# Moving the mask tables, the statistics steps and the fetch depth in the convolution layer of a fused kernel

## The chip, the cores and the metric

The kernel runs on one core of one Trainium2 chip. The metric is the device time of one execution in microseconds (us); lower is better. A core has four compute engines with a queue of instructions each: PE (TensorE, matmuls; its weight loads are listed as PEld), DVE (VectorE), ACT (ScalarE) and POOL (GpSimd). A fifth queue, SP, issues the transfers between DRAM and the core's own memory (SBUF). Matmul results land in banks of a memory of their own (PSUM). Each queue is worked through in the order in which it was built; an instruction whose input or buffer is not ready waits, and what stands behind it waits too.

## The reference

The input x is 128 images x 128 channels x 16 x 16, float32. Two layers are computed:

```
gn(v): group norm, 32 groups of 4 channels
bn(v): batch norm over batch and both image axes
aq(v): round(clip(v, 0, 1) * 15) / 15
# layer 0
h = aq(bn(gn(x)))
h = conv3x3(h, quantised(w1) * cross)           # 5 taps differ from 0
h = aq(bn(h))
h = conv3x3(h, quantised(w2) * diagonal)        # 5 taps differ from 0
x = x + (h + gn(x))
# layer 1, on tokens (16*16 per image, 128 channels)
t = tokens(x)
t = t + mamba(layernorm(t)) + reversed(mamba(reversed(layernorm(t))))
t = t + experts(layernorm(t))                   # 8 experts, the best 2 of each token
```

The mamba has 4 heads and works in chunks of 64 tokens. Inside a chunk it needs a triangular mask, forward and backward. The kernel builds that mask into a small matmul of two tables, `rows` and `cols`, which are constants.

## The kernel before, in words

The images are taken in pairs: one pair is a tile of 128 channels x 2 images x 256 positions, 256 KB, and there are NP = 64 pairs (B = 128 images). Layer 0 comes in three stages, and layer 1 follows as the main stage. The engines' instructions in the layer 0 stages are put in order by a scheduler when the program is built: it simulates when each operand is ready by costs of its own and lets each engine take what is ready first. `issue_after` is a hint to it to hold an instruction back behind another. The main stage has its order written out by hand as a schedule of steps. All loads and stores named here are issued by SP.

**Setup (0 to 87 us).** The first weights w1 are loaded, then all 64 pairs into `xr` (L371), which stay in SBUF through layer 0; after them the weights of layer 1 (`load_weights`, L278 to 307) and w2 (L400, 401). Each image's mean and variance per channel come from `bn_stats` on DVE (L443); every fourth image is instead done by ACT, a sum first (L441) and a sum of squares about the mean later (L457, which needs the mean from L453 to 455). The images are cut into four groups, `cuts` (L414): 0 to 48, 48 to 96, 96 to 120 and 120 to 128. After a group's statistics come small steps on 128 x (images of the group) values: L462 to 468 make the mean and variance of each image and channel, a matmul with `grp` (L472, a table made in L347 to 355) averages over the 4 channels of a norm group, L473 to 476 and a second matmul (L478) make the group variance, L480 adds epsilon and L481 takes the square root on ACT. `normed` (L420 to 434) takes the reciprocal, makes one Newton step and leaves the scale and shift of the group norm; it is called for a group after the statistics of the next. All these small steps are DVE's, but for two in `normed` (L431, L432, GpSimd's: `ares` and `bres`, by which x is scaled in the second convolution). L495 to 511 fold group norm and batch norm into one scale `sc1` and one shift `bi1` for each image and channel.

In the same stage GpSimd makes the two constant tables: `rows0` by 8 copies and `cols0` by 4 copies and 8 selections (`patterns`, L376 to 397, called in L488). L489 and L490 store them to DRAM as `rows_d` and `cols_d` (each 128 x 2048 bf16, 512 KB), from where `constants` (L695 to 698) loads them, three times each, at the beginning of the main stage. The buffers of `rows0` and `cols0` belong to the pool `setup1`, whose space is used by the q buffers of the next stage.

**First convolution (87 to 169 us).** For each pair: ACT or GpSimd makes q = xr * sc1 + bi1 (L525, 527), DVE clips it and writes it as integers into one of four padded images `hpad` (L192, in `quantise`), PE makes 5 matmuls of 128 x 512 (L218, in `conv3x3`), ACT copies the result (L541), DVE takes its statistics for the second batch norm (L542), and SP stores it (L544). The first 8 pairs are not stored but kept in SBUF. `by_weights` (L223) looks at the quantised weights and branches to one of three versions of the stage; with these weights it is the one with 5 taps and one matmul for each.

**Second convolution (169 to 293 us).** For each pair: SP fetches the first result from DRAM (`fetch`, L615 to 618, 6 buffers, issued 5 pairs ahead), ACT scales it (L622) and DVE writes the padded image (L192), PE makes 5 matmuls (L218), the two images in xr are scaled by GpSimd (L665; of every fourth pair one image by ACT, L663), DVE adds the two (L666). `stored` (L625 to 635) transposes the pair before on PE (L631), ACT copies the result to `yt` (L633, 3 buffers) and SP stores it (L635, to y, for layer 1); the first 4 pairs are kept in SBUF instead. The loop is at L649 to 674. Some steps of layer 1's weights (`second_weights`, L309 to 342, with matmuls in L318) and of its first layernorm (`early`, L637 to 645, with ACT's L600) are put between.

**Main stage (293 us to the end).** Mamba and experts. The change does not touch its code.

Of the kernel before, what the change touches and what calls it, by code (L numbers as in the profile page):

```python
# [8 lines left out]
F32 = mybir.dt.float32  # L9
BF16 = mybir.dt.bfloat16  # L10
AF = mybir.ActivationFunctionType
ALU = mybir.AluOpType
AX = mybir.AxisListType

P = 128
NT = 256
# [5 lines left out]
NH = 4  # L22
HD = 64
# [11 lines left out]
def kernel(ctx: ExitStack, tc: tile.TileContext, a: dict):  # L35

    nc = tc.nc
    x_d, out_d = a["x"], a["out"]
    B = x_d.shape[0]
    NP = B // 2  # L40
# [19 lines left out]
    rows_d = dram.tile([P, NH, 2, 2, P], BF16, name="rows_d")  # L60
# [248 lines left out]
    def second_weights(pool, psw):  # L309
# [31 lines left out]
        nc.vector.tensor_scalar(aneg, aneg, -1.0, None, ALU.mult)  # L341
        yield

    with tc.tile_pool(name="w1p", bufs=1) as w1p:

        grp = w1p.tile([P, P], F32, name="grp")
# [5 lines left out]
            out=grp, in_=grp, pattern=[[4, 32], [0, 4]], compare_op=ALU.is_ge, fill=0.0,  # L352
            base=3, channel_multiplier=-1,
        )
        nc.vector.tensor_scalar(grp, grp, 0.25, None, ALU.mult)
        sc1 = w1p.tile([P, B], F32, name="sc1")
        bi1 = w1p.tile([P, B], F32, name="bi1")
        wq1 = w1p.tile([P, 9, 3, P], BF16, name="wq1")
# [1 line left out]
        with tc.tile_pool(name="setup1", bufs=1) as setup, tc.tile_pool(  # L360
# [8 lines left out]

            for i in range(NP):  # L370
                nc.sync.dma_start(xr[i], x_c[:, 2 * i : 2 * i + 2, :])  # L371
            rows0 = setup.tile([P, NH, 2, 2, P], BF16, name="rows0")
            cols0 = setup.tile([P, 2, 2, 2, 2, P], BF16, name="cols0")
            far = setup.tile([HD, 1], BF16, name="far")

            def patterns():  # L376
                nc.gpsimd.memset(far, -1e30)
                for h in range(NH):
                    nc.gpsimd.tensor_copy(
                        rows0[:, h].rearrange("p d t l -> p (d t l)"), heads[:, h : h + 1].to_broadcast([P, 4 * P])  # L380
                    )
                    nc.gpsimd.tensor_copy(
                        rows0[0:HD, h].rearrange("p d t (f l) -> p (d t f) l", l=HD),
                        ident[0:HD, 0:HD].unsqueeze(1).to_broadcast([HD, 2 * 2 * 2, HD]),
                    )
                for m in range(2):
                    for d in range(2):
                        sign = 1 - 2 * d
                        nc.gpsimd.tensor_copy(
                            cols0[:, m, d].rearrange("p j f l -> p (j f l)"), triple[:, m : m + 1].to_broadcast([P, 4 * P])  # L390
                        )
                        for half in range(2):
                            nc.gpsimd.affine_select(
                                out=cols0[0:HD, m, d, :, half, :], in_=far.unsqueeze(2).to_broadcast([HD, 2, P]),
                                pattern=[[0, 2], [sign, P]], compare_op=ALU.is_ge, fill=0.0,
                                base=-sign * HD * half - 1, channel_multiplier=-sign,
                            )

            load_weights()
            w2 = w1p.tile([P, 9, P], F32, name="w2", tag="w")  # L400
            nc.sync.dma_start(w2, a["L0_conv_w2"])


            bst = setup.tile([P, B, 6], F32, name="bst")
# [6 lines left out]
            mean, var, dm, gm, dev, qv, ga, neg, shift = (  # L411
                tb(n) for n in ("mean", "var", "dm", "gm", "dev", "qv", "ga", "neg", "shift")
            )
            cuts = [0, 3 * B // 8, 3 * B // 4, B - max(B // 16, 1), B]  # L414

            def by_scalar(b):

# [2 lines left out]
            def normed(c):  # L420

                of = slice(cuts[c], cuts[c + 1])
                var_, gm_, dev_, ga_, qv_, dm_ = (t[:, of] for t in (var, gm, dev, ga, qv, dm))
                nc.vector.reciprocal(ga_, ga_)
                nc.vector.tensor_tensor(dm_, ga_, ga_, ALU.mult)
                nc.vector.tensor_tensor(dm_, dm_, qv_, ALU.mult)
                nc.vector.tensor_scalar(dm_, dm_, -0.5, 1.5, ALU.mult, ALU.add)
                nc.vector.tensor_tensor(ga_, ga_, dm_, ALU.mult)
                nc.vector.scalar_tensor_tensor(shift[:, of], gm_, -1.0, ga_, ALU.mult, ALU.mult)
                nc.gpsimd.tensor_scalar(ares[:, of], ga_, 1.0, SCALE, ALU.add, ALU.mult)  # L430
                nc.gpsimd.tensor_scalar(bres[:, of], shift[:, of], SCALE, None, ALU.mult)  # L431
                nc.vector.tensor_tensor(dev_, dev_, ga_, ALU.mult)  # L432
                nc.vector.tensor_tensor(var_, var_, ga_, ALU.mult)
                nc.vector.tensor_tensor(var_, var_, ga_, ALU.mult)

            for c in range(4):
                of = slice(cuts[c], cuts[c + 1])
                for b in range(B)[of]:
                    x_b = xr[b // 2][:, b % 2, :]
                    if by_scalar(b):  # L440
                        nc.scalar.activation(junk, x_b, AF.Copy, accum_out=bst[:, b, 1:2])  # L441
                    else:
                        behind = nc.vector.bn_stats(bst[:, b, :], x_b)  # L443
                if c > 0:

                    with tc.issue_after(behind.ins):
                        normed(c - 1)
                mean_, var_, dm_, gm_, dev_, qv_, ga_ = (t[:, of] for t in (mean, var, dm, gm, dev, qv, ga))
                mine = [b for b in range(B)[of] if by_scalar(b)]
                if mine:  # L450

                    picked = slice(mine[0], cuts[c + 1], 4)
                    nc.vector.tensor_scalar(neg[:, picked], bst[:, picked, 1], -1.0 / NT, None, ALU.mult)  # L453
                    nc.vector.tensor_scalar(bst[:, picked, 1], neg[:, picked], -1.0, None, ALU.mult)
                    nc.vector.tensor_scalar(bst[:, picked, 4], neg[:, picked], -1.0, None, ALU.mult)
                    for b in mine:
                        nc.scalar.activation(  # L457
                            junk, xr[b // 2][:, b % 2, :], AF.Square, bias=neg[:, b : b + 1],
                            accum_out=bst[:, b, 2:3],
                        )  # L460

                nc.vector.tensor_tensor(mean_, bst[:, of, 1], bst[:, of, 4], ALU.add)  # L462
                nc.vector.tensor_scalar(mean_, mean_, 0.5, None, ALU.mult)
                nc.vector.tensor_tensor(dm_, bst[:, of, 1], bst[:, of, 4], ALU.subtract)
                nc.vector.tensor_tensor(dm_, dm_, dm_, ALU.mult)
                nc.vector.tensor_tensor(var_, bst[:, of, 2], bst[:, of, 5], ALU.add)
                nc.vector.tensor_scalar(dm_, dm_, 0.25, None, ALU.mult)
                nc.vector.scalar_tensor_tensor(var_, var_, 1.0 / NT, dm_, ALU.mult, ALU.add)

                n = cuts[c + 1] - cuts[c]  # L470
                gm_ps = psa.tile([P, 512], F32, name=f"gm_ps{c}", tag="gm_ps", bufs=2)[:, :n]
                nc.tensor.matmul(gm_ps, grp, mean_, start=True, stop=True)  # L472
                nc.vector.tensor_copy(gm_, gm_ps)  # L473
                nc.vector.tensor_tensor(dev_, mean_, gm_, ALU.subtract)
                nc.vector.tensor_tensor(qv_, dev_, dev_, ALU.mult)
                nc.vector.tensor_tensor(qv_, qv_, var_, ALU.add)
                gv_ps = psa.tile([P, 512], F32, name=f"gv_ps{c}", tag="gv_ps", bufs=2)[:, :n]
                nc.tensor.matmul(gv_ps, grp, qv_, start=True, stop=True)  # L478

                nc.vector.tensor_scalar(qv_, gv_ps, EPS, None, ALU.add)  # L480
                nc.scalar.activation(ga_, qv_, AF.Sqrt)  # L481
                if c == 0:
                    for _ in range(5):
                        next(weights)
                if c == 1:
                    for _ in weights:
                        pass
                    patterns()  # L488
                    nc.sync.dma_start(rows_d, rows0)  # L489
                    nc.sync.dma_start(cols_d, cols0)  # L490
                if c == 3:
                    normed(c)

            bm = setup.tile([P, 1], F32, name="bm")
            nc.vector.tensor_reduce(bm, dev, AX.X, ALU.add)  # L495
# [109 lines left out]
    def conv2(taps, nq):  # L605
        with tc.tile_pool(name="pc", bufs=6) as pc, tc.tile_pool(
# [7 lines left out]

            def fetch(i):  # L615
                if NP > i and i not in kept:
                    qs[i] = pc.tile([P, 2, NT], F32, name=f"q2_{i}", tag="q")
                    nc.sync.dma_start(qs[i], o1_d[i])

            def quantised(i):  # L620
# [16 lines left out]
            def early(i):  # L637
# [6 lines left out]
                nc.scalar.copy(uTs[i], u_ps)  # L644
                yield

            early_steps = [step for i in range(2) for step in [early(i)] * 5]

            for i in range(5):  # L649
                fetch(i)  # L650
            for i in range(3):
                quantised(i)
            for i in range(NP):
                b = 2 * i
                fetch(i + 5)
                if i + 3 < NP:
                    quantised(i + 3)
                ps = psc.tile([P, 2, NT], F32, name=f"cv2_{i}", tag="cv")
# [9 lines left out]
                stored(i - 1)  # L668
                if i >= NP // 2 and early_steps:
                    next(early_steps.pop(0))  # L670
                if i % max(NP // 8, 1) == max(NP // 8, 1) - 1:
                    with tc.issue_after(behind.ins):
                        next(weights, None)
            stored(NP - 1)
            for step in early_steps:
                next(step)
            for _ in weights:
# [634 lines left out]
```

## Time and profile before

| | us |
|---|---|
| median of 3 runs | 2557.53 |
| the 3 runs | 2561.13, 2553.94, 2557.53 |
| the profiled execution | 2554.94 |
| its span, first to last instruction | 2553.1 |

The granted TensorE clock of the profiled execution is 0.991. Busy time of the engines in the stages, in us, with the mean busy share of the 16 DMA engines and what they moved:

| stage, us of the span | PE | DVE | ACT | POOL | DMA share | GB/s |
|---|---|---|---|---|---|---|
| setup, 0 to 87.3 | 6.13 | 65.79 | 42.18 | 23.91 | 0.78 | 237 |
| first convolution, 87.3 to 168.8 | 77.82 | 74.87 | 67.07 | 56.87 | 0.48 | 177 |
| second convolution, 168.8 to 293 | 108.45 | 85.62 | 92.08 | 72.55 | 0.74 | 250 |
| main stage, 293 to 2553 | 2222.88 | 2026.88 | 1971.63 | 1475.98 | 0.41 | 121 |

How to read the lines of the profile that follow. A line of the *timeline* is: start in us, length in us, engine, code line, operation, output<-input with shapes, how many instructions the line stands for, and in brackets the idle time of the engine ahead of it with what ended that. SPq is SP's queue issuing transfers. A line of the *waits* is: engine, what waited and its code line, what it waited for, then the sum of the waits in us, how many, and the longest. The *chain of work that ended last* is followed back from the last instruction, at each step to what released it.

### The profile page before, as it was taken

The numbers are of one execution on the slowest core, as the hardware profiler recorded it, in microseconds if no ns is written. First come the engines' busy times: TensorE is split into PE (matmuls) and PEld (weight loads), VectorE is DVE, ScalarE is ACT, GpSimd is POOL, SyncE is SP. The second block draws the span as 40 slices with busy tenths as digits, with TensorE's granted clock in tenths as the row PEclk, the third lists the DMA queues.
The fourth block names the chain that finished last, engine by engine and source line by source line (L and its number), as shares of the span: only waits on it lengthen the run. The fifth ranks groups of instructions, "written<-read, shape, count | busy, mean of one in ns | idle before, by whom it ended". The sixth has DMA issues, their size and how long they took to land.

```text
span 2553.1 us, 49290 instructions
## 1 busy us (share of the span) xinstructions
PE 2415.3 (95%) x15940; PEld 1479.9 (58%) x15940; DVE 2253.2 (88%) x6163; ACT 2173.0 (85%) x4455; POOL 1629.3 (64%) x1694
## 2 busy tenths in 40 slices
PE   0688889999999999999999999999999999999997
PEld 0235456666666666666666666666666666666663
DVE  8787699999999999999999999999999999999883
ACT  5678699888889998889898888998988899898881
POOL 3468026676666666666666666666667666666666
PEclk9999899999999999999999999999999999999998
DMA  9358633434444444444444344444433443443343
GB/s 287 124 192 281 227 67 110 125 111 123 130 124 122 122 125 118 120 132 128 120 126 124 114 119 129 128 121 119 129 118 117 132 132 121 123 123 116 107 125 107
DMA packets 302167, 339.58 MB, mean 133 GB/s; under 512 B 56768, under 2 KB 226752, under 8 KB 301888
## 3 DMA queue, kind: packets, MB, share of 16 engines
q1 hardware_dynamic: 301888, 336.21, 43.3%
q8 instruction: 133, 2.18, 0.3%
q14 instruction: 146, 1.20, 0.2%
HBM read 262.72 MB, written 56.62 MB: 125 GB/s over the span
## 4 chain that ended last, share of the span: by engine, by line
PE 88%; DMA 4%; DVE 3%; ACT 2%; issue 1%; SPq 1%; POOL 1%; POOLq 0%; ACTq 0%; DVEq 0%
PE f_ps L1189 17%; PE x_ps L877 13%; PE y_ps L1012 10%; PE z_ps L920 9%; PE o_ps L1072 9%; PE sg L965 5%; PE xt_ps L932 4%; PE y_ps L1018 4%; PE g_ps L951 4%; PE cv L218 4%; DMA xr<-in_x 2%; PE n_ps L1045 1%; PE u_ps L1094 1%; PE f_ps L1184 1%; PE u_ps L750 1%
## 5 line engine op out<-in xcount | busy, mean ns | idle before, releaser
L1177 POOL TENSOR_TENSOR gb<-gb,u2T 128x512 f32<-128x512 f32 x512 | 641.3, 1277 | 122.7 <-PE y_ps L1018 68.8
L895 DVE SCALAR_TENSOR_TENSOR xc<-x_ps,cw,xc 128x510 f32<-128x510 f32 (+2 forms) x768 | 571.7, 744 | 46.5 <-ACT xc L889 36.9
L1028 POOL TENSOR_TENSOR yg<-yg,z 128x512 f32<-128x512 f32 x256 | 325.9, 1279 | 352.1 <-DVE yg L1024 155.1
L1189 PE MATMUL f_ps<-gb,ew 128*128 128x512 f32 x1024 | 510.1, 602 | 6.7 <-POOL gb L1177 6.4
L877 PE MATMUL x_ps<-uT,wx 128*128 128x512 f32 x768 | 402.9, 607 | 7.6 <-ACT e L731 3.3
L731 ACT ACTIVATE e<-sg 128x512 f32<-128x512 f32 x512 | 299.3, 591 | 49.9 <-PE sg L965 44.4
L731 ACT ACTIVATE e<-e,ends 128x128 f32<-128x128 f32 x1024 | 325.0, 392 | 0.0
L1012 PE MATMUL y_ps<-e,xt 128*64 128x256 f32 x2048 | 317.8, 389 | 0.2 <-DVE yg L1024 0.2
L993 DVE TENSOR_TENSOR e<-e,g_ps 128x1024 f32<-128x1024 f32 x256 | 311.6, 1217 | 5.5 <-ACT e L731 2.4
L895 DVE SCALAR_TENSOR_TENSOR bc<-x_ps,cw,bc 128x510 f32<-128x510 f32 (+2 forms) x384 | 286.7, 747 | 20.5 <-ACT bc L889 4.1
L1189 PEld LDWEIGHTS f_ps<-gb,ew 128*128 128x128 f32 x1024 | 180.5, 192 | 174.2 <-issue 136.2
L920 PE MATMUL z_ps<-uT,wz 128*128 128x512 f32 x512 | 271.2, 611 | 1.5 <-ACT xc L889 1.0
L889 ACT ACTIVATE xc<-x_ps,cb,cw 128x512 f32<-128x512 f32 x256 | 199.0, 777 | 64.0 <-PE x_ps L877 57.4
L1072 PE MATMUL o_ps<-wo,yg 128*128 128x128 f32 x2048 | 251.4, 276 | 0.2 <-DVE e L998 0.2
L1072 PEld LDWEIGHTS o_ps<-wo,yg 128*128 128x128 f32 x2048 | 240.5, 193 | 11.1 <-DVE g L1149 8.4
L1024 DVE SCALAR_TENSOR_TENSOR yg<-xc,dcol,y_ps 128x512 f32<-128x512 f32 x256 | 189.8, 742 | 50.1 <-PE y_ps L1018 46.8
L1060 POOL TENSOR_TENSOR rr<-rr,mhalf 128x8 f32<-128x8 f32 x64 | 109.9, 1718 | 161.7 <-DVE g L1151 82.7
L1018 PE MATMUL y_ps<-e,xt 128*64 128x128 f32 x2048 | 199.0, 273 | 0.0
L965 PE MATMUL sg<-rows,cols 128*128 128x256 bf16 x1024 | 192.1, 274 | 5.8 <-ACT e L731 2.8
L1018 PEld LDWEIGHTS y_ps<-e,xt 128*64 128x64 f32 x2048 | 147.0, 137 | 74.1 <-DVE e L998 0.5
L218 PE MATMUL cv<-hpad,wq 128*128 128x512 bf16 x640 | 161.7, 396 | 19.5 <-DVE hpad L192 19.4
L1012 PEld LDWEIGHTS y_ps<-e,xt 128*64 128x64 f32 x2048 | 118.9, 136 | 100.9 <-issue 53.8
(256 smaller groups left out, 4813.9 us busy)
## 6 DMA issues: line engine op xcount, KB each, us to landing
gb<-gd SPq DMA_DIRECT2D x256, 512.0 KB
e<-cum SPq DMA_DIRECT2D x256, 256.0 KB
xr<-in_x SPq DMA_DIRECT2D x64, 256.0 KB
cc<-bc SPq DMA_DIRECT2D x128, 128.0 KB
out<-ob SPq DMA_DIRECT2D x64, 256.0 KB
y<-yt SPq DMA_DIRECT2D x60, 256.0 KB
yt<-y SPq DMA_DIRECT2D x60, 256.0 KB
o<-o SPq DMA_DIRECT2D x56, 256.0 KB
```

Of the source, the lines that this page charges most:

```text
L731: nc.scalar.activation(out, in_, func, **more)
L877: nc.tensor.matmul(ps, wx[d][:, n * P : (n + 1) * P], uTs[i], start=True, stop=True)
L895: nc.vector.scalar_tensor_tensor(acc[:, :, to], raw[:, :, of], cw[:, d, n, 3 - back : 4 - back], acc[:, :, to], ALU.mult, ALU.add,)
L920: nc.tensor.matmul(ps, wz[:, d, n * P : (n + 1) * P], uTs[i], start=True, stop=True)
L965: nc.tensor.matmul(sg[:, :, of], c_[:, k, d, s, half, :], r_[:, :, d, s, of], start=True, stop=True)
L993: nc.vector.tensor_tensor(e0.rearrange("p h t l -> p h (t l)"), e0.rearrange("p h t l -> p h (t l)"), gps[i, d, k][:, 0:NT].unsqueeze(1).t ...
L1012: nc.tensor.matmul(y_ps[64 * q : 64 * q + 64, k, :], xt[:, 2 * k + s0, 64 * h : 64 * h + 64], e0[:, h].rearrange("p t l -> p (t l)"), star ...
L1018: nc.tensor.matmul(y_ps[64 * q : 64 * q + 64, k, s1 * P : (s1 + 1) * P], xt[:, 2 * k + s1, 64 * h : 64 * h + 64], e1[:, h, :], start=False ...
L1028: large(nc.gpsimd.tensor_tensor(yg, yg, zs[i, d][:, n, :], ALU.mult))
L1072: nc.tensor.matmul(o_ps[:, (2 * j + d) * P : (2 * j + d + 1) * P], ygs[i, d, n][:, t * P : (t + 1) * P], wo[d][:, n, :], start=(n == 0), s ...
L1177: large(nc.gpsimd.tensor_tensor(gb[:, e], gb[:, e], u2Ts[i], ALU.mult))
L1189: nc.tensor.matmul(f_ps, ew[:, e, :], gbs[i, e], start=False, stop=(e == NE - 1))
```

## The change

Four things are changed.

1. `patterns` becomes a generator that takes a pool. It is no longer called in the setup, but in the second convolution: from pair 32 on, one of its steps is put into the program after each pair, and what is left after the last pair. Its three tables (`rows0`, then `cols0` in two halves) use one buffer in turn (tag "table", bufs=1), so that the stores are now one of 512 KB to `rows_d` and two of 256 KB to `cols_d`, each of which must have read the buffer before the next table is made.
2. The small steps of the first batch norm are issued by GpSimd for the first three groups, by DVE for the last; the copy of the group means out of PSUM (L473) by ACT for the first three groups. Two `scalar_tensor_tensor` instructions become two instructions each. The scaling of `grp` goes to GpSimd. `normed` is called directly after each group. The third bound of `cuts` goes from image 120 to 112.
3. The q buffers of the second convolution go from 6 to 10, and the fetches from 5 to 8 pairs ahead.
4. The load of w2 is issued ahead of `load_weights` instead of behind it.

```diff
+    def patterns(pool):
+        far = pool.tile([HD, 1], BF16, name="far", bufs=1)
+        nc.gpsimd.memset(far, -1e30)
+        rows0 = pool.tile([P, NH, 2, 2, P], BF16, name="rows0", tag="table", bufs=1)
+        for h in range(NH):
+            nc.gpsimd.tensor_copy(
+                rows0[:, h].rearrange("p d t l -> p (d t l)"), heads[:, h : h + 1].to_broadcast([P, 4 * P])
+            )
+            yield
+            nc.gpsimd.tensor_copy(
+                rows0[0:HD, h].rearrange("p d t (f l) -> p (d t f) l", l=HD),
+                ident[0:HD, 0:HD].unsqueeze(1).to_broadcast([HD, 2 * 2 * 2, HD]),
+            )
+            yield
+        nc.sync.dma_start(rows_d, rows0)
+        for m in range(2):
+            cols0 = pool.tile([P, 2, 2, 2, P], BF16, name=f"cols0_{m}", tag="table", bufs=1)
+            for d in range(2):
+                sign = 1 - 2 * d
+                nc.gpsimd.tensor_copy(
+                    cols0[:, d].rearrange("p j f l -> p (j f l)"), triple[:, m : m + 1].to_broadcast([P, 4 * P])
+                )
+                yield
+                for half in range(2):
+                    nc.gpsimd.affine_select(
+                        out=cols0[0:HD, d, :, half, :], in_=far.unsqueeze(2).to_broadcast([HD, 2, P]),
+                        pattern=[[0, 2], [sign, P]], compare_op=ALU.is_ge, fill=0.0,
+                        base=-sign * HD * half - 1, channel_multiplier=-sign,
+                    )
+                    yield
+            nc.sync.dma_start(cols_d[:, m], cols0)
...
-        nc.vector.tensor_scalar(grp, grp, 0.25, None, ALU.mult)
+        nc.gpsimd.tensor_scalar(grp, grp, 0.25, None, ALU.mult)
...
-            load_weights()
             w2 = w1p.tile([P, 9, P], F32, name="w2", tag="w")
             nc.sync.dma_start(w2, a["L0_conv_w2"])
+            load_weights()
...
-            cuts = [0, 3 * B // 8, 3 * B // 4, B - max(B // 16, 1), B]
+            cuts = [0, 3 * B // 8, 3 * B // 4, 7 * B // 8, B]
+            half_ = setup.tile([P, B], F32, name="half_")
...
+                eng = nc.vector if c == 3 else nc.gpsimd
                 nc.vector.reciprocal(ga_, ga_)
-                nc.vector.tensor_tensor(dm_, ga_, ga_, ALU.mult)
...
+                eng.tensor_tensor(dm_, ga_, ga_, ALU.mult)
...
-                if c > 0:
-
-                    with tc.issue_after(behind.ins):
-                        normed(c - 1)
...
-                    nc.vector.tensor_scalar(neg[:, picked], bst[:, picked, 1], -1.0 / NT, None, ALU.mult)
+                    nc.gpsimd.tensor_scalar(neg[:, picked], bst[:, picked, 1], -1.0 / NT, None, ALU.mult)
...
-                nc.vector.tensor_tensor(mean_, bst[:, of, 1], bst[:, of, 4], ALU.add)
+                eng.tensor_tensor(mean_, bst[:, of, 1], bst[:, of, 4], ALU.add)
...
-                nc.vector.tensor_copy(gm_, gm_ps)
+                (nc.vector.tensor_copy if c == 3 else nc.scalar.copy)(gm_, gm_ps)
...
-                    patterns()
-                    nc.sync.dma_start(rows_d, rows0)
-                    nc.sync.dma_start(cols_d, cols0)
-                if c == 3:
-                    normed(c)
+                normed(c)
...
-                    qs[i] = pc.tile([P, 2, NT], F32, name=f"q2_{i}", tag="q")
+                    qs[i] = pc.tile([P, 2, NT], F32, name=f"q2_{i}", tag="q", bufs=10)
...
+            tables = patterns(pc)
...
-            for i in range(5):
+            for i in range(8):
                 fetch(i)
...
-                fetch(i + 5)
+                fetch(i + 8)
...
+                if i >= NP // 2:
+                    with tc.issue_after(behind.ins):
+                        next(tables, None)
...
             stored(NP - 1)
+            for _ in tables:
+                pass
```

The other lines of the diff send further small steps of `normed` and of the group loop, in the same way, to `eng`.

## The prediction

> **What bounds the kernel now.** I read the page first. PE is busy 95% of the span and the chain of work that ended last is 88% PE, nearly all of it in the main stage, which the change does not touch: from 293 us on, the instructions of all engines are the same in both built programs, apart from two memsets that change places. So I read the 293 us ahead of it: the chain and the timeline from 65 to 92 us for the join of batch norm and first convolution (conv1), then waits, GpSimd's and the DMA queue's timelines from 178 to 293 us for the second convolution (conv2).
>
> ```profile
> 11.14 7.84 DVE L355 TENSOR_SCALAR grp<-grp 128x128 f32<-128x128 f32 x1
> 17.43 1.48 POOL L393 TENSOR_SCALAR_AFFINE_SELECT cols<-far 64x256 bf16<-64x256 bf16 x4
> ...
> 77.33 0.29 DVE L511 TENSOR_SCALAR bi<-bi,b 128x128 f32<-128x128 f32 x1
> 79.74 0.43 SPq L489 DMA_DIRECT2D rows_d<-rows  x1
> 85.72 3.23 ACT L525 ACTIVATE q<-xr,bi,sc 128x256 f32<-128x256 f32 x6 [13.64 <-DMA rows_d<-rows]
> 87.33 4.97 PE L218 MATMUL cv<-hpad,wq 128*128 128x512 bf16 x13 [11.41 <-DVE hpad L192]
> ```
>
> The scale and shift for conv1 are ready at 77.62, but its first q tile lies where the tables lay, and waits until they are copied out at 85.72. Between them 8.1 us are lost; PE starts at 87.33.
>
> ```profile
> ACT q L622 <- DMA q<-o: 13.7, 16, 1.5
> PEld yt_ps L631 <- ACT yt L633: 9.6, 13, 1.2
> ```
>
> These waits of conv2 say that its image pairs come late from DRAM.
>
> ```profile
> 177.77 35.92 POOL L665 TENSOR_SCALAR xr<-xr,ares,bres 128x256 f32<-128x256 f32 x59 [4.39 <-issue]
> ...
> 216.30 4.36 POOL L665 TENSOR_SCALAR xr<-xr,ares,bres 128x256 f32<-128x256 f32 x7
> ...
> 222.36 0.55 POOL L665 TENSOR_SCALAR xr<-xr,ares,bres 128x256 f32<-128x256 f32 x1
> ...
> 223.26 25.52 POOL L665 TENSOR_SCALAR xr<-xr,ares,bres 128x256 f32<-128x256 f32 x42
> ```
>
> GpSimd scales xr without a pause and never waits for the convolution: 59 instructions in 35.92 us, 0.609 each. It is through pair 39 (the 70th instruction) at 222.9, 45.1 us after it began, and done at 248.8.
>
> ```profile
> 186.17 2.55 SPq L618 DMA_DIRECT2D q<-o  x2
> ...
> 187.53 0.58 ACT L633 ACTIVATE yt<-yt_ps 128x512 f32<-128x512 f32 x1
> ...
> 188.82 0.38 SPq L635 DMA_DIRECT2D y<-yt  x1
> ...
> 198.58 0.32 SPq L635 DMA_DIRECT2D y<-yt  x1
> ```
>
> The store of pair 4 is ready at 188.11 and leaves at 188.82, right behind a fetch that had to wait for a buffer: the DMA queue keeps its order. The last line is the store of pair 10.
>
> [...] conv1's first matmuls take 622 ns, later ones 404.
>
> **Setup.** GpSimd loses 20 table instructions and gets grp, so VectorE starts on the images at 11.2 instead of 18.9. But SP delivers a pair each 0.7525 us (ScalarE's waits at 10.16, 11.66, ..., 25.21 for every second pair), the last at 10.16 + 62 x 0.7525 = 56.8, and the small steps now go VectorE, ScalarE, GpSimd, PE and back, in queues that keep order. I followed these queues in the built order. A GpSimd step costs 0.29 (L430 to L431: 72.70 to 72.99). Group 1's squares end on ScalarE near 57.5; four GpSimd steps 1.2, matmul 0.66, so VectorE's epsilon step (L480), in front of the last nine image statistics, runs at 59.5 although it was reached some 6 us earlier; square root, reciprocal, 60.5. GpSimd's queue then holds 25 steps, the rest of group 1 and the statistics of group 2: 7.3, to 67.8. Matmul, L480, root and reciprocal 1.6: 69.4. VectorE's last group took 8.67 before (68.95 to 77.62) and is alike: 78.1. So the small steps gain nothing; what the earlier start gives, new waits take. VectorE's branch takes 1.85 (171.36 to 173.21), hpad and PE's start 0.8: PE starts at 80.8, not 87.33. Gain 6.5. Bounds: at 0.20 per step (smallest L430) 3 us better, at 0.61 (largest) 8 worse: gain -1.5 to 9.5. Weights in another order (w2 0.67 us earlier, the rest later by that, two table stores gone): nothing, since ScalarE needs w2 after conv1's first tiles and the rest is used past 200 us; without that cover 0.67. Conv1 itself: PE-bound before (77.8 of 81.5 us busy) and after, so 0.
>
> **Conv2: fetches.** Ten buffers and eight pairs ahead replace six and five. A pair takes 1.545 us of PE where nothing waits (the chain late in conv2 goes on in steps like 280.28 to 281.83), so 3 more pairs are 4.6 us against a wait of 1.5 at most. From pair 16 (207.04) to 63 (292.35) before: 85.3 = 47 x 1.545 + 12.7. Of the 12.7, 5.4 are work: two 1.1 us matmuls L318 and two times 1.6 for L600. The other 7.3 are waits for fetches and what they cause; I take 5.9 as saved, since 512 KB per 1.545 us are 339 GB/s, where 320 made a DMA share of 0.92. Bounds 0 to 7.3.
>
> **Conv2: tables.** In the built order the tables are not beside idle time. GpSimd makes rows0 between the xr steps of pairs 32 to 39; its store stands in SP's queue right after the store of pair 10 and ahead of stores 11, 12 and all fetches from 26 on. So SP must stand from store 10 (20.8 us after GpSimd's start: 198.58 - 177.77) until GpSimd is past pair 39. That is 45.1 + 8 casts x 0.58 (L379, L382: 1.16 for two) + 0.1 = 49.8; less 1.6, as some 20 of its steps fall into a standstill of VectorE and cost 0.52 (214.69 to 215.21): 48.2. Who waits: yt has three buffers, so ScalarE stops at yt of pair 14, which needs store 11; PE has two banks for yt_ps and stops before the transposes of pair 15, at about 27 us. At 48.2 SP sends rows_d (512 KB, 1.5 us) and store 11; landing 5.1 (0.9 issue, 0.6 of the table still ahead, and the 3.6 that the chain shows for a y store at 247.51), yt 0.6: PE goes on at 53.9. It then has 48 steps of 1.545 to pair 63, 74.2, its transposes 0.6, work 5.4, leftover waits 1.4[...]. Sum 137.2, where before it was 115.2 (177.77 to 292.98). Cost net of the fetches' gain: 22.0.
>
> The two cols_d stores wait for cols0, which GpSimd makes after all xr steps, at 48.2 + 42 x 0.608 + 2.7 = 76.5[...]. Hidden by 3.5 us and by three yt buffers more; without that cover some 4 each. rows_d and cols_d are read by the main stage's first loads, 30 us later: 0.
>
> **Sum.** Profiled execution 2554.94 (span 2553.1 and 1.84 around it) - 6.5 + 22.0 = 2570.4. The median of the runs, 2557.53, lies 2.6 above the profiled one; I take 2571.
>
> **Rivals.** (1) As above, 2571: 0.57. (2) The cols stores bite too, 4 us each: GpSimd, [...] slower than 0.7 us per xr step, or PE faster to pair 30. 2571 + 8 = 2579: 0.13. (3) The standstill is there but short: setup gains 9.5, GpSimd keeps to 0.52 sooner (44 instead of 48.2), the restart finds no leftover waits (1.4): 2571 - 3 - 4.2 - 1.4 = 2562: 0.21. (4) Faster: the store of rows_d does not stop SP, since rows0 is ready when SP arrives. From yt's three buffers the point is 20.8 + 3 x 1.545 = 25 us after GpSimd's start. Then -6.5 and, with the first 16 pairs' 2.6 as well, -5.9 - 2.6: 2556 - 15 = 2541. For it: the order was made by a scheduler which must have thought rows0 ready at pair 10. Against it: 70 xr steps in 25 us would be 0.36 each, and the shortest shown is 0.52. 0.09.
>
> **Numbers.** Measurement can tell about 0.3%, 7.7 us, from no change: 2549.9 to 2565.2. Faster is (4), 0.09; within is (3), 0.21; slower (1) and (2), 0.70. The range takes in (1), (2) and most of (3): the setup's bounds (-3, +8), the fetches' (-1.4, +5.9) and 4 for the cols stores, not all at once: 2558 to 2584.
>
> **What would show it.** Right: conv1's first matmul near 80.8 with no wait for rows_d; in conv2 one hole in PE of about 27 us with SP's rows_d issue at its end, ScalarE waiting for a y store, GpSimd busy throughout; from pair 16 steps of 1.545; main stage shifted by 15. Wrong: stores of pairs 11 and 12 issued before rows_d, no hole, or GpSimd's small steps moving conv1's start past 87.

## The result, and the profile after

| | before | changed |
|---|---|---|
| median of the runs, us | 2557.53 (2553.94 to 2561.13) | 2569.34 (2568.70 to 2572.18) |
| ratio to before, 95% interval | | 1.0049 [1.0034, 1.0063] |
| profiled execution, us | 2554.94 | 2569.89 |
| its span, us | 2553.1 | 2568.0 |

The changed kernel is slower by about 12 us. The two spans differ by 14.9 us, and the traces say where they lie. "T" is the moment at which GpSimd starts to scale xr in the second convolution (conv2), 177.77 before and 170.23 after.

| stretch, from the traces, us | before | changed | difference |
|---|---|---|---|
| start to the first matmul of conv1 | 87.33 | 81.70 | -5.6 |
| from there to conv1's end (first L210 for conv2) | 81.55 | 80.86 | -0.7 |
| from there to T | 8.89 | 7.67 | -1.2 |
| T to the last transposes of conv2 | 115.21 | 136.68 | +21.5 |
| main stage | 2260.1 | 2261.1 | +1.0 |

First the join of setup and conv1, from the timeline of the changed kernel (all engines, lines left out between). It answers to the last four lines of the first block in the prediction.

```profile
77.02 0.28 DVE L514 TENSOR_SCALAR bi<-bi,b 128x128 f32<-128x128 f32 x1
...
77.47 3.06 ACT L528 ACTIVATE q<-xr,bi,sc 128x256 f32<-128x256 f32 x6 [5.68 <-DVE bi L514]
...
81.70 13.65 PE L218 MATMUL cv<-hpad,wq 128*128 128x512 bf16 x53 [6.29 <-DVE hpad L192]
```

The first q tile now follows the shift at once (77.30 to 77.47), where before it waited for the tables' store until 85.72. But the shift itself is no earlier than before (77.62).

Then SP's timeline in conv2. L638 is the store of a transposed pair, L621 the fetch, L359 the store of rows_d, L375 those of cols_d.

```profile
190.50 0.32 SPq L621 DMA_DIRECT2D q<-o  x1
191.72 0.32 SPq L638 DMA_DIRECT2D y<-yt  x1
218.69 0.32 SPq L359 DMA_DIRECT2D rows_d<-rows  x1
219.10 1.22 SPq L638 DMA_DIRECT2D y<-yt  x2
220.41 0.59 SPq L621 DMA_DIRECT2D q<-o  x1
...
252.30 0.38 SPq L621 DMA_DIRECT2D q<-o  x1
252.77 0.44 SPq L375 DMA_DIRECT2D cols_d<-cols  x1
...
260.00 0.32 SPq L638 DMA_DIRECT2D y<-yt  x1
260.42 0.38 SPq L375 DMA_DIRECT2D cols_d<-cols  x1
```

From 192.04 to 218.69 SP issues nothing: 26.65 us. It stands at the rows_d store, with the ready stores of pairs 11 and 12 and all fetches behind it. At the cols_d stores it does not stand. GpSimd's timeline in the same stretch shows what SP waits for:

```profile
170.23 34.76 POOL L669 TENSOR_SCALAR xr<-xr,ares,bres 128x256 f32<-128x256 f32 x58 [3.11 <-issue]
...
204.97 0.60 POOL L350 CAST rows<-heads 128x512 bf16<-128x512 f32 x1
...
218.06 0.60 POOL L354 CAST rows<-ident 64x512 bf16<-64x512 f32 x1
218.65 25.09 POOL L669 TENSOR_SCALAR xr<-xr,ares,bres 128x256 f32<-128x256 f32 x42
```

The last piece of rows0 ends at 218.66, and SP goes on at 218.69. Next the waits of the changed kernel from conv1's end to the start of the main stage (sum in us, number, longest), and below them PE's line at its restart:

```profile
ACT yt L636 <- DMA y<-yt: 25.6, 2, 25.0
ACT q L625 <- DMA q<-o: 7.8, 13, 1.2
```

```profile
222.76 1.11 PE L634 MATMUL yt_ps<-ident,xr 128*128 128x128 f32 x4 [23.20 <-ACT yt L636]
223.66 2.34 PE L218 MATMUL cv<-hpad,wq 128*128 128x512 bf16 x5
...
226.65 1.78 PE L218 MATMUL cv<-hpad,wq 128*128 128x512 bf16 x5
...
228.71 1.27 PE L218 MATMUL cv<-hpad,wq 128*128 128x512 bf16 x5
```

ScalarE waits 25 us for a yt buffer, that is for a y store which SP has not issued; PE waits 23.2 us for ScalarE and then starts slowly: its matmuls on a pair take 0.634 us each at first, at a granted clock of 0.50, and 0.378 from 227.84 on, at 1.00 (medians). The clock was 1.00 from 200 to 202 and 0.50 from 204 to 222, while PE waited. The slow stretch lasted 5.1 us; from the transposes at 222.76 to the next at 225.80 and at 228.27 it is 3.04 and 2.47 us where later pairs take 1.545, together 2.4 more. The kernel before has such a start at its first matmuls of conv2: 0.634 us at 0.50 from 174.74 on, 0.378 at 1.00 from 180 on. Its first matmuls of conv1, the 622 ns in the prediction, came at a granted clock of 1.00. This is the hole that was foreseen, with 23.2 us somewhat shorter than the 27 expected.

### The profile page after: what moved, and what is told of

It is laid out like the page before. It is cut to its first block, busy times and chain, and to the rows that moved or that the text cites. A ratio compares the mean times of both kernels' runs of the same rounds, so it can differ in the third digit from the quotient of the medians.

```text
span 2568.0 us, 49304 instructions
## 1 busy us (share of the span) xinstructions
PE 2416.4 (94%) x15940; PEld 1482.0 (58%) x15940; DVE 2237.4 (87%) x6100; ACT 2170.6 (85%) x4450; POOL 1647.1 (64%) x1764
## 4 chain that ended last, share of the span: by engine, by line
PE 87%; DVE 3%; DMA 3%; POOL 3%; ACT 2%; issue 1%; SPq 0%; POOLq 0%; DVEq 0%; ACTq 0%
PE f_ps L1198 17%; PE x_ps L886 13%; PE y_ps L1021 9%; PE z_ps L929 9%; PE o_ps L1081 9%; PE sg L974 5%; PE xt_ps L941 4%; PE y_ps L1027 4%; PE g_ps L960 4%; PE cv L218 3%; DMA xr<-in_x 2%; POOL xr L669 2%; PE n_ps L1054 1%; PE f_ps L1193 1%; PE u_ps L1103 1%
```

## The experiments

Theory A is the prediction's: SP stands at the rows_d store and through three yt buffers stops ScalarE and PE. Theory B is that GpSimd's added work in conv2 costs the time wherever the store stands. Each ratio is against the kernel before, timed on the same chip. The runs were spread over several chips, on which the kernel before had medians of 2555.80 to 2557.71, so differences of medians between kernels can be off by some 2 us. conv2 is the stretch from T to the last transposes in the profiled execution, the hole PE's longest wait in it (none: no wait over 1.5 us).

| kernel | median us | ratio [95%] | conv1 starts | conv2 | hole |
|---|---|---|---|---|---|
| before | 2557.53 | | 87.33 | 115.2 | none |
| changed | 2569.34 | 1.0049 [1.0034, 1.0063] | 81.70 | 136.7 | 23.2 |
| store_behind_39 | 2550.26 | 0.9977 [0.9968, 0.9986] | 81.36 | 114.0 | none |
| store_behind_20 | 2557.01 | 1.0002 [0.9994, 1.0010] | 81.60 | 123.5 | 6.5 |
| store_by_gpsimd | 2558.63 | 1.0011 [0.9999, 1.0022] | 81.81 | 123.7 | 6.1 |
| rows_made_early | 2564.00 | 1.0024 [1.0015, 1.0032] | 81.72 | 119.4 | 2.1 |
| rows_early_again | 2562.28 | 1.0018 [0.9989, 1.0046] | 81.88 | 132.1 | 10.4 |
| six_yt_buffers | 2574.24 | 1.0068 [1.0055, 1.0081] | 81.61 | 141.8 | 24.5 |
| after_fetch_old | 2575.36 | 1.0071 [1.0057, 1.0084] | 81.56 | 141.3 | 23.4 |
| fetch_alone | 2555.05 | 0.9995 [0.9988, 1.0002] | 88.33 | 112.7 | none |
| half_fetches | 2545.97 | 0.9956 [0.9943, 0.9969] | 81.76 | 111.6 | 3.0 |
| tables_apart | 2550.45 | 0.9974 [0.9964, 0.9984] | 82.06 | 116.0 | 2.0 |
| small_steps_vector | 2565.89 | 1.0033 [1.0020, 1.0046] | 75.83 | 136.0 | 21.8 |
| late_store_vector | 2547.41 | 0.9961 [0.9948, 0.9973] | 76.14 | 120.3 | 4.2 |

Stretches whose instructions are the same in all these programs differ between profiled executions too: conv1 from 80.9 to 82.7 us, the main stage from 2260.1 to 2264.6. A difference of one stage below 2 us is therefore not read from a single trace.

### Where the store of rows_d stands: store_behind_39 and store_behind_20

```diff
-        nc.sync.dma_start(rows_d, rows0)
+        with tc.issue_after(sent[39]):
+            nc.sync.dma_start(rows_d, rows0)
...
+            for _ in range(6):
+                yield
+            with tc.issue_after(sent[(50, 62)[m]]):
+                nc.sync.dma_start(cols_d[:, m], cols0)
...
-                    nc.sync.dma_start(y_d[i], yt)
+                    sent[i] = nc.sync.dma_start(y_d[i], yt).ins
```

`sent[20]` in place of `sent[39]` makes the second kernel. Here the hint names an instruction of SP, a y store, and the table store stands behind it. In the changed kernel the same hint names an instruction of VectorE, and the store went into SP's queue right behind the store of pair 10, long before.

> The changed kernel, but the store of rows_d is put into SP's queue behind the y store of pair 39 and the cols_d stores behind pairs 50 and 62; nothing else is changed. Theory A (SP stands at the rows_d store behind pair 10 and stops the pipeline): no stop, so the 25 us hole in PE goes and conv2 takes about 109 us from GpSimd's start instead of 136.7: 2569.3 - 27.4 = 2542. Theory B (the cost is GpSimd's added work in conv2[...], the place of the store is incidental): the hole goes but the time comes back elsewhere, 2560 or more. Theory C (A is right, but the deeper fetch brings little): 2545 to 2548.

> The changed kernel, but the rows_d store stands behind the y store of pair 20 instead of pair 10. Theory A: SP reaches it 10 pairs of 1.545 us later, while GpSimd finishes rows0 at the same time (48.4 us after its start), so the hole in PE shrinks from 25 by 15.4 to about 9.6 us: 2569.3 - 15.4 = 2554. Theory B: no dose effect, 2560 or more whatever the place.

Measured: 2550.26 and 2557.01, against 2569.34. SP's and PE's timelines of store_behind_20 (y stores are L644, fetches L627 there):

```profile
210.14 0.41 SPq L627 DMA_DIRECT2D q<-o  x1
221.95 0.32 SPq L362 DMA_DIRECT2D rows_d<-rows  x1
```

```profile
226.06 1.11 PE L640 MATMUL yt_ps<-ident,xr 128*128 128x128 f32 x4 [6.51 <-ACT yt L642]
```

SP stands 11.4 us instead of 26.65. Against store_behind_39, in which SP doesn't stand, the two standstills cost 6.7 and 19.1 us by the medians, and 9.5 and 22.7 by conv2 in the single traces (123.48 and 136.68 against 113.96). By theory A the three yt buffers hide 3 x 1.545 = 4.6 us, which leaves 6.8 and 22.0: right to some 3 us. So the cost grows with the time that SP stands, and theory B falls, since GpSimd makes the same tables in all three. The 2554 expected of store_behind_20 was missed by 3; rows0 was ready 51.0 us after T there, not 48.4. And 2550.26 is not 2542. The hole is gone and conv2 is still 114.0, hardly less than the 115.2 of before. That is beyond even theory C's 2545 to 2548: A holds, and the deeper fetch brings little.

### The stores on another queue, and the table earlier: store_by_gpsimd, rows_made_early, rows_early_again

```diff
-        nc.sync.dma_start(rows_d, rows0)
+        nc.gpsimd.dma_start(rows_d, rows0)
...
-            nc.sync.dma_start(cols_d[:, m], cols0)
+            nc.gpsimd.dma_start(cols_d[:, m], cols0)
```

> The changed kernel, but GpSimd's own queue issues the three table stores, at once after it has made each table; SP has none. Theory A: as with the stores late in SP's queue, about 2542, no hole in PE. GpSimd waits for the rows_d store before it makes cols, but by then its scaling of xr is done, so that costs nothing. Theory B: 2560 or more. If the issue by GpSimd costs it time or holds VectorE, some us more than the run with the late stores.

The other kernel lets the tables start at pair 0 and leaves the rows_d store to the scheduler, with the cols_d stores behind pairs 50 and 62:

```diff
-                if i >= NP // 2:
+                if i < 8 or i >= NP // 2:
                     with tc.issue_after(behind.ins):
                         next(tables, None)
```

> The changed kernel, but rows0 is made beside pairs 0 to 7 and not 32 to 39; its store stands even earlier in SP's queue than in the changed kernel, ahead of the first y store; the cols_d stores stand behind pairs 50 and 62. Theory A (what stops SP is that rows0 is not ready, not where the store stands): rows0 is ready some 13 us after GpSimd's start, SP gets there at about 11, the three yt buffers hide the rest: no hole, 2550 to 2553 (up to 3 us more than store_behind_39, since the first pairs' xr comes later from GpSimd). Rival (a store of 512 KB in the middle of the queue, or its place as such, costs the time): 2560 or more.

> The same kernel as rows_made_early, whose runs were mostly 2563 to 2566 while its profiled execution took 2555.7 and showed no hole: looked at once more, in the hope of an execution of the usual length. Theory H (VectorE is held off by GpSimd): one VectorE step of some 0.42 us lasts 6 to 9 us, as 7.63 in store_by_gpsimd and 5.72 in late_store_vector, beside GpSimd instructions that follow one another without a pause; PE waits for it. Rival (SP): SP stands longer at the rows_d store, and ScalarE waits for a y store or a fetch for some 8 us more than in the first profile.

Measured: 2558.63 and 2564.00, both above what theory A gave, and with executions from 2549.9 to 2570.1 and from 2549.8 to 2567.4 more scattered than any other kernel here. In the profiled execution of rows_made_early, one of its short ones, SP waits for rows0 for 10 us near the start and PE has no hole over 2.1 us: this standstill makes no hole, as theory A says. Its conv2 is still 5.4 us longer than that of store_behind_39, in many short waits; what causes them was not found. In the longer executions time is lost in another way, which the profile of rows_early_again shows. VectorE, GpSimd and PE in rows_early_again (each from its own timeline):

```profile
182.87 11.02 DVE L192 TENSOR_SCALAR hpad<-q 128x512 uint8<-128x512 f32 x1
```

```profile
182.62 1.08 POOL L674 TENSOR_SCALAR xr<-xr,ares,bres 128x256 f32<-128x256 f32 x2
183.66 0.60 POOL L356 CAST rows<-ident 64x512 bf16<-64x512 f32 x1
184.25 15.93 POOL L674 TENSOR_SCALAR xr<-xr,ares,bres 128x256 f32<-128x256 f32 x28
```

```profile
195.21 1.09 PE L639 MATMUL yt_ps<-ident,xr 128*128 128x128 f32 x4 [10.38 <-DVE xr L675]
```

A VectorE step that takes 0.425 us in the median of its 120 lasts 11.02 us beside GpSimd instructions without a pause, and PE waits 10.4 us for it. The same in store_by_gpsimd:

```profile
234.96 7.63 DVE L192 TENSOR_SCALAR hpad<-q 128x512 uint8<-128x512 f32 x1
```

So what theory H expected is what these executions show, and the rival (SP standing longer) is not; that GpSimd is what holds VectorE is inferred from the overlap. That it explains the usual length of rows_made_early is shown for one execution only, and that of store_by_gpsimd likewise; why these two kernels meet it so often is open.

### Who is stopped by SP: six_yt_buffers

```diff
-                yt = yts[i] if i in yts else pc.tile([P, 4, P], F32, name=f"yt_{i}", tag="yt", bufs=3)
+                yt = yts[i] if i in yts else pc.tile([P, 4, P], F32, name=f"yt_{i}", tag="yt", bufs=6)
```

(and the same number where `early` uses these buffers), on top of after_fetch_old.

> after_fetch_old (six q buffers, five pairs ahead) with six yt buffers instead of three. Theory A's chain: with SP standing behind pair 10, ScalarE stops at the yt that needs the store of pair 11; three buffers more let PE run three pairs of 1.545 us further, so the hole shrinks by 4.6: 2575.4 - 4.6 = 2570.8. Rival: what stops PE is the missing fetches, which SP does not issue either: no change, 2575.

Measured 2574.24 against 2575.36: no gain that can be told. Its waits in conv2:

```profile
ACT q L625 <- DMA q<-o: 38.4, 17, 23.7
```

With more yt buffers ScalarE no longer stops at a y store. It stops a little later at a fetch, 23.7 us, which SP doesn't issue either; with six q buffers that limit lies close behind the first. The rival was right, and beside six q buffers the yt buffers alone are not a remedy. With ten, as in the changed kernel, they were not tried.

### What the deeper fetch is worth: fetch_alone, after_fetch_old, half_fetches

fetch_alone is the kernel before with this part of the change alone; after_fetch_old is the changed kernel with it undone (the same lines the other way).

```diff
-                    qs[i] = pc.tile([P, 2, NT], F32, name=f"q2_{i}", tag="q")
+                    qs[i] = pc.tile([P, 2, NT], F32, name=f"q2_{i}", tag="q", bufs=10)
...
-            for i in range(5):
+            for i in range(8):
...
-                fetch(i + 5)
+                fetch(i + 8)
```

> The kernel before with only the fetch part of the change: ten q buffers in conv2 and eight pairs ahead. The prediction's step: 5.9 us less (bounds 0 to 7.3), so 2551.6; conv2's waits of ScalarE for a fetch (13.7 us in sum) mostly gone. Rival: DRAM sets the pace of conv2, the waits come back as others, 2556 to 2557.5.

> The changed kernel with the fetch part undone: six q buffers, five pairs ahead. If the deeper fetch brought the 5.9 us that the prediction took off: 2575.2, more ScalarE waits for fetches after the standstill. Rival: beside the standstill of SP the fetch depth is worth nothing, 2569 to 2571.

half_fetches is store_behind_39 with the following, by which the odd pairs from 9 on, 28 in all, are not fetched; it computes something else and serves only to ask what the fetches cost:

```diff
-                if NP > i and i not in kept:
+                if NP > i and i not in kept and i % 2:
+                    qs[i] = kept[i // 2 % 8]
+                elif NP > i and i not in kept:
```

> store_behind_39, but conv2 leaves out the fetch of every even pair from 8 on and takes one of the eight kept tiles instead, so that its input for these pairs is not the first convolution's result. It asks why fetching ahead brought 1.3 to 3.4 us where the prediction took off 5.9. Theory A2 (the pace of DRAM transfers, 272 to 295 GB/s in conv2, bounds the pairs, not the depth of the queue): with 28 fetches fewer the waits of ScalarE for q (12.2 us) go, and conv2 from GpSimd's start falls from 114 to 107 to 109, so 2550.3 - 6 = 2544. Theory B2 (the waits are from buffers or order): 2549 to 2551.

Measured: alone the deeper fetch gains 0.0005 [-0.0002, 0.0012] of the time, 1.3 us, no gain that is sure, and in the trace conv2 shrinks by 2.5 us (115.2 to 112.7). Undone in the changed kernel it costs 6.0 us by the medians (2575.36 - 2569.34), 5.6 by the ratios, much as the prediction had it, and conv2 grows by 4.6. So its worth seems to depend on the standstill. The waits of fetch_alone and of store_behind_39 in conv2, one line each, show that what it was to remove is still there without one:

```profile
ACT q L622 <- DMA q<-o: 10.0, 12, 1.5
```

```profile
ACT q L631 <- DMA q<-o: 12.2, 14, 1.5
```

Before it was 13.7: ScalarE waits for fetches nearly as long with ten buffers as with six. Busy time in a stretch of conv2 (PE, PEld, VectorE, ScalarE, GpSimd, each with its number of instructions, then PE's clock, the DMA engines' share and GB/s), for store_behind_39, half_fetches and, after its hole, the changed kernel:

```profile
200.00:228.00 28.00, 25.21 (x140) 14.42 (x139) 22.27 (x34) 25.23 (x43) 28.00 (x48) 1.00 0.85 282
```

```profile
200.00:228.00 28.00, 27.84 (x156) 16.36 (x155) 24.54 (x38) 28.00 (x48) 28.00 (x46) 1.00 0.70 227
```

```profile
222.80:250.00 27.20, 25.90 (x132) 14.99 (x132) 19.18 (x29) 24.46 (x42) 24.09 (x41) 0.91 0.92 310
```

With 28 fetches left out, no wait for a fetch is left, PE is busy 27.84 of 28 us from 200 to 228, and conv2 takes 111.6. The time falls by 4.3 us by the medians, 5.4 by the ratios (the two intervals just touch), where 6 were expected; 3.0 us are one wait of PE near 245, for VectorE, which was then at a row of steps for layer 1's weights. So the waits for fetches do cost about what theory A2 said. That the pace of the transfers is their reason is not shown, and two things in the traces speak against it. The same transfers ran at 282 GB/s in store_behind_39 and at 310 in the changed kernel, so 282 was no ceiling. And PE is not short of pairs. Matching each fetch with ScalarE's step on the same pair and with PE's first matmul on it, for pairs 20 to 63, gives:

| kernel | fetch issued to ScalarE's step, median us | from there to PE, median (least) us |
|---|---|---|
| before | 4.0 | 10.5 (8.0) |
| fetch_alone | 4.3 | 16.7 (11.2) |
| store_behind_39 | 4.3 | 16.9 (10.0) |
| half_fetches, fetched pairs | 15.8 | 23.2 (11.3) |

ScalarE scales a pair at least 8 us before PE takes it. A fetch leaves when a buffer comes free, behind y stores that SP waits for, and ScalarE's step on the same pair follows in its queue some 4 us later, before the data are there. With ten buffers both moved forward together, by four or five pairs, and the 4 us between them stayed. PE is then held indirectly: of the 11.0 us for which it waits in fetch_alone for ScalarE's copies to yt, 7.3 come within 3 us of such a wait of ScalarE. This points to the order of ScalarE's queue, which is theory B2. half_fetches can't decide between the two, since leaving out fetches also frees buffers and brings the remaining ones 15.8 us ahead; a kernel that takes ScalarE's step later in its queue would, and was not run. That a standstill makes depth worth more, because PE then restarts with ten fetched pairs in hand instead of six, is argued from the numbers, not shown.

### The setup: tables_apart and small_steps_vector

tables_apart is the kernel before with the tables at the end of the setup's space, and conv1's pool told to wait for a tile's own space rather than for the whole of it (the three lines move down from where they stood, behind the loads of xr):

```diff
+            rows0 = setup.tile([P, NH, 2, 2, P], BF16, name="rows0")
+            cols0 = setup.tile([P, 2, 2, 2, 2, P], BF16, name="cols0")
+            far = setup.tile([HD, 1], BF16, name="far")
             cuts = [0, 3 * B // 8, 3 * B // 4, B - max(B // 16, 1), B]
...
-            with tc.tile_pool(name="pb", bufs=3) as pb, tc.tile_pool(
+            with tc.tile_pool(name="pb", bufs=3, reuse_waits="tile") as pb, tc.tile_pool(
```

> The kernel before, tables made and stored in the setup as before, but in space that the first q tiles of conv1 do not use, so that conv1 need not wait for their stores. If the wait for rows_d and cols_d was what stood between bi1 (77.6) and conv1, PE starts at about 81 instead of 87.3 and the time is 2557.5 - 6.5 = 2551. Rival: the stores hold up conv1 in another way (the load queue is full until then), or the gain of the changed kernel's setup came from GpSimd's small steps: 2557.

small_steps_vector is the changed kernel with the lines of before for the small steps, `cuts` and the place of `normed`, and no tables there (three of the lines that differ):

```diff
-                eng = nc.vector if c == 3 else nc.gpsimd
...
-                eng.tensor_tensor(mean_, bst[:, of, 1], bst[:, of, 4], ALU.add)
+                nc.vector.tensor_tensor(mean_, bst[:, of, 1], bst[:, of, 4], ALU.add)
...
-                normed(c)
+                if c == 3:
+                    normed(c)
```

> The changed kernel with the small steps of the first batch norm as they were (VectorE, old cuts, normed after the next group's statistics), the tables in conv2. Step of the prediction: the small steps on GpSimd gain nothing, so bi1 is ready within 1 us of the changed kernel's 77.3 and the time is 2569.3 +- 1.5. Rival: the GpSimd steps are what brought conv1's start from 87.3 to 81.7; then it goes back by up to 5.6 us, 2575.

Measured: tables_apart 2550.45, as expected (2551). Its timeline:

```profile
77.42 0.29 DVE L511 TENSOR_SCALAR bi<-bi,b 128x128 f32<-128x128 f32 x1
77.79 3.06 ACT L525 ACTIVATE q<-xr,bi,sc 128x256 f32<-128x256 f32 x6 [5.62 <-DVE bi L511]
...
80.75 0.43 SPq L489 DMA_DIRECT2D rows_d<-rows  x1
...
82.06 8.16 PE L218 MATMUL cv<-hpad,wq 128*128 128x512 bf16 x28 [6.33 <-DVE hpad L192]
```

The store goes out at 80.75, after ScalarE has begun, and nobody waits for it. The wait for the tables' space was the loss at this join. What the tables cost in the setup otherwise, this kernel leaves as it was: the shift is ready at 77.71, as before.

small_steps_vector missed what was expected of it. The shift was ready at 71.97 instead of 77.30 and conv1 started at 75.83 instead of 81.70:

```profile
71.68 0.29 DVE L514 TENSOR_SCALAR bi<-bi,b 128x128 f32<-128x128 f32 x1
```

The rival had the size (5.9 us against its 5.6) with the sign turned round: the new form of the steps did not bring conv1's early start, it kept it from being earlier. Two lines of VectorE and one of GpSimd in the changed kernel show where:

```profile
57.78 0.31 POOL L473 TENSOR_TENSOR var<-bst 128x48 f32<-128x48 f32 x1 [5.56 <-ACT junk L463]
...
59.99 0.21 DVE L487 TENSOR_SCALAR qv<-gv_ps 128x48 f32<-128x48 f32 x1 [5.99 <-PE gv_ps L485]
...
68.02 0.17 DVE L487 TENSOR_SCALAR qv<-gv_ps 128x16 f32<-128x16 f32 x1 [3.92 <-PE gv_ps L485]
```

VectorE stands 5.99 and 3.92 us at the epsilon step, with its last image statistics behind it. The first wait is mostly for ScalarE's sums of squares, for which GpSimd waits 5.56 us too; its own four steps and a matmul take the last 2.2. The second is for GpSimd, which works through two groups' steps in turn. In small_steps_vector VectorE waits 0.37 us at most at these steps, since image statistics stand ahead of them. As engine, cuts and the place of `normed` were put back together, how much each of them cost is open.

### The two repairs together: late_store_vector

It is small_steps_vector with the stores of store_behind_39.

> Both repairs together: the table stores late in SP's queue (behind pairs 39, 50, 62) and the small steps of the first batch norm on VectorE as before; tables in conv2 and the deep fetch stay. Conv1 should start at about 75.8 as in small_steps_vector, conv2 should have no hole as in store_behind_39: 2550.3 less what the small steps gave in the run before, 3.4 (2569.3 - 2565.9, medians) to 5.9 (81.70 - 75.83, the start of conv1): 2544 to 2547. Rival: what is gained ahead of conv1 comes back in conv2, which then is short of data: 2549 to 2550.

Measured 2547.41, 0.9961 [0.9948, 0.9973] of before: by its median the fastest kernel here that computes the whole, with an interval that overlaps those of store_behind_39 and tables_apart. It lies at the edge of the 2544 to 2547 expected. Conv1 starts at 76.14, but conv2 takes 120.3, so part of the gain is lost again. PE waits 4.2 us in it, again for one long VectorE step:

```profile
215.49 5.72 DVE L192 TENSOR_SCALAR hpad<-q 128x512 uint8<-128x512 f32 x1
```

## Why the prediction was right, and where it was not

**The sum.** Predicted 2571 (2570.4 for the profiled execution), measured 2569.34 (2569.89). The sign, the place and the main mechanism, the standstill of SP, were as foreseen. One step, the fetches, was wrong without showing in the sum.

**Setup.** Predicted: shift at 78.1, PE at 80.8, gain 6.5. Measured 77.30, 81.70, 5.6. "What the earlier start gives, new waits take" is what the trace has, down to the epsilon step at 59.99 (59.5 foreseen) and the next group's reciprocal, done at 68.7 (69.4 foreseen). I then misread my own step in the expectation for small_steps_vector: that steps gain nothing on balance does not mean that undoing them changes nothing. In their new form, with cuts and order, they cost 5.9 us of conv1's start. What else changed ahead of conv1 had brought the shift forward by 5.7 (77.62 to 71.97): the tables and grp's scaling off the two queues, by which VectorE starts on the images at 11.2 instead of 18.9, and w2's place, which was not tried alone.

**Standstill.** Times from T, predicted and measured: SP stops at 20.8 and 21.8, rows0 is ready at 48.2 and 48.4, PE goes on at 53.9 and 52.5, conv2 ends at 137.2 and 136.7. PE stopped at 29.3 and not at 27, so the hole was shorter; what followed it took 84.2 instead of 83.3. The 83.3 holds an allowance for PE's slow restart, the author's estimate; by the step times above the restart cost 2.4 us. ScalarE stopped where it was expected, at a yt that needs a store behind rows_d.

**The cols_d stores.** Predicted hidden, with GpSimd ready at 76.5 and SP there, behind store 30, at 80 for the first (with the same allowance in it). Measured 76.7 and 82.5. The second was hidden by only 0.5 us (ready at 259.88, issued at 260.42), so rival 2 was near.

**Fetches: the step that failed.** "The other 7.3 are waits for fetches and what they cause; I take 5.9 as saved." The reading under it was wrong: ScalarE's 13.7 us of waits were taken to say that pairs come late from DRAM, which more depth would mend. They came at least 8 us before PE took them, and late only for ScalarE's own step, which moves forward with the fetch. Without a standstill ten buffers save 2.5 us of conv2 (1.3 us by the ratio). What holds the rest is not settled; it was seen to go with the fetches. The prediction also set the cost of the standstill 5 us too high: 22.0 + 5.9 = 27.9 against a conv2 without waits for fetches, where store_behind_39 gives 22.7. The two errors cancel, 27.9 - 5.9 against 22.7 - 1.2 (115.2 - 114.0). This is not mere luck: the conv2 with the hole was worked out directly (137.2), and the one without it was not needed for the sum. They do not cancel in rival 4: its 2541 is what store_behind_39 makes real, and that took 2550.26, 9 us more.

**Conv1 and main stage.** Predicted unchanged; -0.7, -1.2 ahead of T, and +1.0 are within what equal stretches differ by.

## What to carry to other kernels

A transfer that waits for a late producer stops everything behind it in its queue (SP stood 26.65 us at the rows_d store), so the place of a new store in the built order has to be read against the time at which its producer is really done; here moving it behind later stores was worth 19 us, more than any other part of the change. When a wait is removed, ask whether the buffer was the reason or only the place where it showed: the setup's wait was for the tables' space, and conv2's waits for fetches stayed with ten buffers, because the step that waits moved forward with the fetch. Before a deeper queue is counted as a gain, ask when the engine that bounds the stage needs the data. And steps moved to an idle engine can still lose, if they are links in a chain through queues that keep their order, as the waits of 5.99 and 3.92 us suggest.

## What the runs showed of the hardware that was not expected

A VectorE step can last many times its usual length while GpSimd works without a pause. A step of L192, 0.42 us in the median, lasted 11.02, 7.63 and 5.72 us, in which 19, 14 and 10 whole GpSimd instructions went by, those on xr of about 0.55 us each. The step of 7.63 us ended at 242.59, 0.39 us into two GpSimd instructions on xr that took 1.34 us together, where nine of them ahead had taken 4.86. The 7.84 us line in the prediction's first block was already of this kind: 15 whole GpSimd instructions went by, and it ended at 18.98, just after the last of GpSimd's tables (18.91). That GpSimd is the cause is inferred from this overlap. It happened in some executions and not in others of the same kernel (one of rows_made_early at 2555.7 us had none over 2.6 us, a longer one had 11.02 and 5.79), and in the profiled executions of the other kernels the longest L192 step took 2.6 to 3.5 us. What decides it is open.
